# A fused convolution, attention and mixture-of-experts kernel: GpSimd in the planner's clock, and the experts' products summed by halves

## The chip, the cores and the metric

The kernel runs on one core of a Trainium2 chip. A core has a matrix engine (TensorE, PE in the profile, with its weight loads as PEld), a vector engine (VectorE, DVE), a scalar engine for activation functions (ScalarE, ACT), a general engine (GpSimd, POOL) and a queue engine that issues DMA transfers (SyncE, SP). Each engine executes its own instructions in the order in which they were written; engines wait for each other on semaphores. Operands lie in the on-chip memory SBUF (128 partitions) or in the accumulator banks of PSUM, which TensorE writes. The metric is device time in microseconds (us), the median of several runs.

## The reference, cut to what matters

The input is four images of 64 x 64 pixels and 128 channels. Layer 0 is a gated residual block with two 3 x 3 convolutions and a strictly causal attention over the 4096 pixels of an image; layer 1 is 16-head attention without a mask over the same 4096 tokens, a gated feed-forward network of width 344, and a mixture of experts in which each token takes the best 2 of 8 experts:

```python
# layer 0
c1 = conv_same(jax.nn.elu(x), W1, b1)
c2 = conv_same(c1, W2, b2)
a, b = jnp.split(c2, 2, axis=-1)
c3 = a * jax.nn.sigmoid(b)
# ... attention with q, k of 4 columns and v of 16, added to c3
# layer 1, t = tokens
scores = jnp.einsum('bqhd,bkhd->bhqk', q, k)      # 16 heads of 8
probs = jax.nn.softmax(scores, axis=-1)
attn = jnp.einsum('bhqk,bkhd->bqhd', probs, v)
h = x + attn @ wo
ffn = jax.nn.silu(h @ w1) * (h @ w3) @ w2
# experts
top_p, top_i = jax.lax.top_k(router_probs, 2)
expert_out = jnp.einsum('bnd,edc->bnec', x, expert_w) + expert_b
out = jnp.einsum('bnk,bnkc->bnc', top_p, jnp.take_along_axis(expert_out, top_i[..., None], axis=2))
```

The largest work is the exponential of layer 1's scores: 4 images x 16 heads x 4096 x 4096.

## The kernel before, in words

**Attention steps.** Tokens are cut into 8 chunks of 512 queries and 32 tiles of 128 keys, heads into 4 groups of 4. A *segment* is one image, group and chunk; it goes over up to 32 key tiles. A step of a segment is one key tile for four heads: four score matmuls on TensorE into two PSUM tiles (`s`, of three in rotation), two exponentials of 128 x 1024 on ScalarE (`e<-s`), and four value matmuls that add to a PSUM sum (`acc<-e,vg`). The value matmuls of a step are issued two steps later.

**Polynomial beside.** In segments that go over all 32 key tiles, key tile 20 is not given to ScalarE. Class `Beside` (L930) computes its exponential on VectorE: per head a score matmul into the single bank `m` (`m<-qx,f_kx`), a scaling out of the bank (`ey<-m`), and then eight SBUF operations of 128 x 512 (`em<-ey`, `eg<-em,ey`, `em<-em`, `ey<-eg`, three of `ey<-ey,eg`, and last `ey<-ey,em`). The eight wait in a list, `beside_todo`, and are issued a few at a time by `beside_work`. When all four heads are done, two *half products* (`half`; `acc<-ey,vg` in the profile, four matmuls each) add the tile to the sum. `rested` (L936 to L949) lets them begin only after two turns have passed since then.

**Fillers.** Between the steps the loop inserts pieces of other work through the same bank `m`: the next image's convolutions (in Winograd form: GpSimd makes the row terms `r` and column terms `v`, and the sums `both` and `less`; VectorE takes the products out of the bank as `sd`, `sums`, `t`), layer 0's attention, the queries and keys of layer 1, and the *last part* of a finished chunk (`last_part`, L1057): output projection, feed-forward network, normalization, router and experts. In the experts' stage each of a chunk's four token tiles gets two bank-fulls of products of four experts each; VectorE multiplies them by their gates into `by_e` (128 x 8 x 128), and then sums over the experts: one `tensor_reduce` on a rearranged view, so that its innermost step is 128 elements, into `added`, which is added to `t`.

**What sets the order.** The order of every engine is written out by hand in one loop (its last lines are L1490 to L1494). A pass is a *turn*, booked at 1.81 us (`turn_at`). Each turn issues one attention step, at most an insertion or two (a filler piece, a unit or a half product of the polynomial), the values of an older step, and then polynomial operations as long as VectorE's booked time `dve_at` stays under `turn_at + 2.5`. The function `dve_time` (L140) moves `dve_at` on with every VectorE operation by an estimate of its duration, and `bank_at` with those that read the bank `m`; pieces that need the bank are inserted only when `bank_at` has passed. GpSimd has no such clock. The clocks exist only while the program is built. Class `InOrder` (L93) records every operation through one line, L113, so in the profile all of them have that line, and groups are told apart by the names of their tiles.

At the end, when no attention step is left, the remaining fillers (here the last parts of the last two chunks) run alone: this is the *tail*.

Of the kernel before, what the change touches and what calls it, by code (L numbers as in the profile page):

```python
# [12 lines left out]
ALU = mybir.AluOpType  # L13
AX = mybir.AxisListType

P = 128
C = 128
# [10 lines left out]
NSLOT = P // SLOT  # L28
# [97 lines left out]
def fast_path(ctx: ExitStack, tc: tile.TileContext, a: dict, where: dict, out: bass.AP, verdict):  # L126
# [6 lines left out]
    nc = tc.nc  # L133
    x = a["x"]
    B = x.shape[0]
    pe, act, pool, sp = (InOrder(tc, e) for e in (nc.tensor, nc.scalar, nc.gpsimd, nc.sync))

    turn_at, dve_at, bank_at = [0.0], [0.0], [0.0]

    def dve_time(name, args):  # L140

        aps = [x for x in args if hasattr(x, "shape")]
        from_bank = any(x.name.startswith("m_") or x.name == "m" for x in aps)
        from_sums = any(x.name.startswith("acc") for x in aps)
        in_sbuf = not any(x.space == bass.MemoryType.PSUM for x in aps)
        took = max(int(np.prod(x.shape[1:])) for x in aps[:2]) / 960.0
        if in_sbuf and name in ("tensor_scalar", "tensor_copy"):
            took *= 0.5
        if name == "tensor_reduce" and aps[1].ap[-1][0] != 1:
            took *= 1.8  # L150
        begins = turn_at[0] + (0.95 if from_bank else 1.75 if from_sums else 0.0)
        dve_at[0] = max(dve_at[0], begins) + 0.07 + took
        if from_bank:
            bank_at[0] = dve_at[0]

    dve = InOrder(tc, nc.vector, dve_time)

    const = ctx.enter_context(tc.tile_pool(name="f_const", bufs=1))
    big = ctx.enter_context(tc.tile_pool(name="f_big", bufs=1))
# [11 lines left out]
    def m_tile():  # L171
        return ps_m.tile([P, QB], FP, tag="m", name="m")
# [7 lines left out]
    def chunk(tag, name=None):  # L180
        return wk.tile([P, QB], FP, tag=tag, bufs=CHUNKS.get(tag, 1), name=name or tag)
# [4 lines left out]
    def by_k(ap):  # L186
        return ap.rearrange("p (k c) -> p k c", k=4)
# [4 lines left out]
    def bank():  # L192
        return s_tile()[:, :QB] if alone[0] else m_tile()
# [153 lines left out]
    def halves(ps, lhs, rhs, size=P):  # L347

        for h in range(2):
            cols = slice(h * QB // 2, (h + 1) * QB // 2)  # L350
            product(ps[:size, cols], lhs, rhs[:, cols])
            if h == 0:
                yield 0.46, "held"
# [576 lines left out]
    class Beside:  # L930


        def __init__(self, seg, n, qx, vg):
            self.seg, self.kt, self.qx, self.vg = seg, seg.beside[n], qx, vg
            self.place = 8 * seg.place(self.kt // 8) + self.kt % 8
            self.e, self.units, self.halves, self.ready, self.rested, self.age = [], 0, 0, 0, 0, 0  # L936
            self.due = [2 + 3 * i for i in range(NSLOT)] + [22, 24]

        def can(self):
            if self.units < NSLOT:  # L940
                return len(beside_todo) < 10
            return self.halves < 2 and self.ready == NSLOT and self.rested > 1

        def late(self):
            return self.age > self.due[self.units + self.halves]

        def step(self):
            self.age += 1
            self.rested += self.ready == NSLOT  # L949

        def piece(self):
            if self.units < NSLOT:
# [6 lines left out]
        def unit(self, j):  # L959
            ps = m_tile()  # L960
            r = slice(j * SLOT, (j + 1) * SLOT)
            pe.matmul(
                ps,
                lhsT=kx[r, self.place * P : (self.place + 1) * P].bitcast(FR),
                rhs=self.qx[r, :].bitcast(FR),
                start=True,
                stop=True,
            )
            y = chunk("ey")
            self.e.append(y)  # L970
            dve.tensor_scalar(y, ps, LOG2E, None, ALU.mult)
            low, a = [], [-((-1) ** k) * POWER[k] / float(np.float32(POWER[5])) for k in range(5)]

            def round_off():
                low.extend([chunk("em"), chunk("part", "eg")])
                dve.tensor_scalar(low[0], y, TO_WHOLE + EXPONENT, None, ALU.add)

            def fraction():
                dve.scalar_tensor_tensor(low[1], low[0], TO_WHOLE + EXPONENT, y, ALU.subtract, ALU.subtract)

            def to_power():
                whole = low[0].bitcast(mybir.dt.int32)
                dve.tensor_scalar(whole, whole, 23, MANTISSA, ALU.logical_shift_left, ALU.bitwise_or)

            def first():
                dve.scalar_tensor_tensor(y, low[1], a[4], low[1], ALU.add, ALU.mult)

            def term(k):
                return lambda: dve.scalar_tensor_tensor(y, y, a[k], low[1], ALU.add, ALU.mult)

            def last():
                dve.scalar_tensor_tensor(y, y, a[0], low[0], ALU.add, ALU.mult)
                self.ready += 1

            beside_todo.extend([(0.35, round_off), (0.6, fraction), (0.35, to_power), (0.6, first)])
            beside_todo.extend([(0.6, term(3)), (0.6, term(2)), (0.6, term(1)), (0.6, last)])

        def half(self, h):
# [7 lines left out]
                    stop=False,  # L1006
                )

    def beside_work(until):
        while beside_todo and dve_at[0] + beside_todo[0][0] <= until:  # L1010
            beside_todo.pop(0)[1]()

    def beside_rest(seg):
# [43 lines left out]
    def last_part(b, c):  # L1057
# [30 lines left out]
        for m in range(4 * len(FCH)):  # L1088
            k, n = divmod(m, len(FCH))
# [25 lines left out]
        shape = [P, 4, NE]  # L1115
# [48 lines left out]
        for k in range(4):  # L1164
            tk = t[:, k * C : (k + 1) * C]
            by_e = wk.tile([P, NE, C], FP, tag="two", bufs=1, name="by_e")
            for half in range(2):
                ps = bank()
                yield from halves(ps, yT[:, k * P : (k + 1) * P], we_f[:, half * QB : (half + 1) * QB])
                dve.tensor_tensor(  # L1170
                    by_e[:, 4 * half : 4 * half + 4, :],
                    by_k(ps),
                    gate[:, k, 4 * half : 4 * half + 4].unsqueeze(2).to_broadcast([P, 4, C]),
                    ALU.mult,
                )
                if half == 1:
                    added = chunk("w", "added")[:, :C]
                    dve.tensor_reduce(added, by_e.rearrange("p e c -> p c e"), AX.X, ALU.add)
                    dve.tensor_tensor(tk, tk, added, ALU.add)
                fetch_following(b, c)  # L1180
                yield 0.46, "stop"
        ps = bank()
# [157 lines left out]
    jobs = []  # L1340
# [107 lines left out]
    while True:  # L1448
        turn_at[0] += EXPS
        if steps_in:  # L1450
            do_step(steps_in.pop(0))
        else:
            step = next(steps, False)
            if step is False:
                break
            waiting = step is None
            if waiting:
                finish(0)
            else:
                do_step(step)  # L1460
        b = now[0]
        if batches[b].second == NQ and len(batches) == b + 1 and b + 1 < B:
            Batch(b + 1)
            begun = 0
            while begun < len(fillers) and (fillers[begun][2] in fetching or fillers[begun][2] is None):
                begun += 1
            fillers.insert(begun, [first_attention(b + 1, batches[b + 1]), PREPARE, None, False])

        rate = 1.0
        if batches[b].second == NQ:  # L1470
            later = PREPARE * (B - len(batches)) + LAST * (last_parts_left[0] - 1)
            rate = (sum(part[1] for part in fillers) + later) / max(1, sum(steps_left) - 40)
        credit = min(3.0, credit + rate)
        left = ahead + EXPS - SCORES - (VALUES if len(undone) > 2 else 0.0)
        free = bool(fillers) and fillers[0][3]
        turn = not quiet[0] and free and not waiting
        if turn:
            took = insert()
            credit -= took
            left -= took  # L1480
        can = [job for job in jobs if job.can() and (left >= PIECE or job.late())]
        empty = bank_held[0] or bank_at[0] <= turn_at[0] + 0.5 or batches[b].second < NQ
        if can and empty and not (quiet[0] or bank_held[0] or steps_in or waiting):
            can[0].piece()
            left -= PIECE
        elif not turn and (waiting or not quiet[0] and empty and credit > 0.0 and (left >= PIECE or credit > 1.5)):
            took = insert()
            credit -= took
            left -= took
        ahead = min(max(left, 0.0), AHEAD)  # L1490
        finish(2)
        for job in jobs:
            job.step()
        beside_work(turn_at[0] + 2.5)  # L1494
    finish(0)
    alone[0] = True
    run_alone([(r for part in fillers for r in part[0])], lambda: False)
# [717 lines left out]
```

## Time and profile before

| what | value |
|---|---|
| median of 4 runs | 8134.53 us (8131.57 to 8137.83) |
| profiled execution, its own time | 8133.86 us |
| its span, first to last instruction | 8132.0 us |
| mean granted TensorE clock | 0.989 of full |
| ScalarE busy; of it the exponentials `e<-s` | 7690.2 us; 7624.5 us in 8256 instructions |
| TensorE busy | 7854.2 us |
| VectorE busy; of it `added<-by_e` | 4902.3 us; 256.0 us in 128 instructions |
| GpSimd busy | 675.4 us |
| ScalarE idle before `e<-s`, until `s` was there | 199.5 us in 132 waits, the longest 13.9 |

A line of the groups reads: source line, engine, operation, output tile `<-` input tiles, partitions x elements, `x` count, then busy us and mean ns of one, then the idle time of the engine just before them and what ended it. A line of the timeline reads: start in us from the start of the span, duration, engine, line, operation, tiles, `x` the number of instructions merged into it; in brackets the idle time before it and what ended it. `s<-qx,f_kx` are the score matmuls, `acc<-e,vg` the value matmuls, `m<-...` every product that goes through the bank `m`.

### The profile page before, as it was taken

The page shows a single profiled execution, that of the slowest core. Times are in us where ns is not written, and L with a number is a line of the kernel's source. Part 1 is how long each engine was busy: PE and PEld are TensorE (multiplying, and loading weights), DVE is VectorE, ACT ScalarE, POOL GpSimd, SP SyncE. Part 2 cuts the span into 40 slices and gives each one's busy share as a digit, 9 for nine tenths or more (in the row PEclk, how much of TensorE's full clock was granted, in tenths as well). Part 3 has the DMA queues.
Part 4 walks back from the last instruction along what each step waited for, and adds up shares of the span by engine and source line. Part 5 has one row for each costly group of instructions (what it writes and reads, how often), then busy time and mean ns, then how long its engine had stood idle before and what let it go on. Part 6 is the DMA issues. An engine that isn't in the chain of part 4 may idle for free. (4 is left out here: it accounts for less than half of the span.)

```text
span 8132.0 us, 177112 instructions
## 1 busy us (share of the span) xinstructions
PE 7854.2 (97%) x73465; PEld 2454.5 (30%) x73465; DVE 4902.3 (60%) x9033; ACT 7690.2 (95%) x8459; POOL 675.4 (8%) x592
## 2 busy tenths in 40 slices
PE   7999999999999999999999999999999999999997
PEld 3232222223322222333322222223233333333333
DVE  4333556463666766656666766666666666666666
ACT  1899999999999999999999999999999999999995
POOL 1211211100012111000001211000000000000000
PEclk9999999999999999999999999999999999999998
DMA  2221010111100101111010011101101111111221
GB/s 72 67 68 65 26 55 31 56 34 61 37 29 13 48 25 42 35 43 39 24 39 28 18 43 42 48 25 47 33 23 55 51 45 49 58 51 44 71 79 33
DMA packets 332338, 356.53 MB, mean 44 GB/s; under 512 B 146083, under 2 KB 222339, under 8 KB 331523
## 3 DMA queue, kind: packets, MB, share of 16 engines
q1 hardware_dynamic: 327507, 343.35, 13.4%
q8 instruction: 578, 9.47, 0.5%
q10 hardware_dynamic: 4016, 1.77, 0.1%
q14 instruction: 237, 1.94, 0.1%
HBM read 209.24 MB, written 135.79 MB: 42 GB/s over the span
## 5 line engine op out<-in xcount | busy, mean ns | idle before, releaser
L113 ACT ACTIVATE e<-s 128x1024 f32<-128x1024 f32 x8256 | 7624.5, 1086 | 208.9 <-PE s L113 199.5
L113 PE MATMUL acc<-e,vg 128*9 128x512 f32 x31872 | 4228.8, 596 | 1.6 <-DVE at L113 1.6
L113 PE MATMUL s<-qx,f_kx 32*128 32x512 f32 (+2 forms) x16512 | 2674.6, 496 | 38.2 <-DMA f_kx<-d_k 20.7
L113 PEld LDWEIGHTS s<-qx,f_kx 32*128 32x128 f32 (+1 forms) x16512 | 1082.3, 182 | 3886.2 <-ACT e L113 3619.2
L113 DVE SCALAR_TENSOR_TENSOR ey<-ey,eg 128x512 f32<-128x512 f32 x1344 | 954.8, 710 | 37.4
L113 PEld LDWEIGHTS acc<-e,vg 128*9 128x9 f32 x31872 | 726.0, 90 | 797.9 <-issue 405.4
L113 PE MATMUL m<-v,f_wino 128*32 128x256 f32 x5376 | 432.9, 394 | 44.6 <-DVE sd L113 25.5
L113 DVE COPY at<-acc 128x512 f32<-128x512 f32 x131 | 90.6, 692 | 621.3 <-PE acc L113 613.0
L113 DVE TENSOR_SCALAR ey<-m 128x512 f32<-128x512 f32 x448 | 306.4, 684 | 56.8 <-PE m L113 53.8
L113 PE MATMUL m<-f_we,y2T 128*32 128x256 f32 x3840 | 308.0, 393 | 28.7 <-DVE by_e L113 28.7
L113 DVE SCALAR_TENSOR_TENSOR eg<-em,ey 128x512 f32<-128x512 f32 x448 | 323.4, 722 | 13.3
L113 DVE SCALAR_TENSOR_TENSOR ey<-ey,em 128x512 f32<-128x512 f32 x448 | 321.1, 717 | 9.9
L113 POOL TENSOR_TENSOR rs<-ve,f_minus_half 128x4 f32<-128x4 f32 x64 | 65.2, 1018 | 3138.0 <-DVE ve L113 3138.0
L113 DVE SCALAR_TENSOR_TENSOR ey<-eg 128x512 f32<-128x512 f32 x448 | 320.7, 716 | 0.0
L113 POOL TENSOR_TENSOR v<-r 128x1024 f32<-128x1024 f32 x112 | 219.6, 1967 | 1132.2 <-PE m L113 1131.8
L113 DVE COPY sd<-m 128x512 f32<-128x512 f32 x168 | 115.8, 689 | 278.4 <-PE m L113 277.7
L113 DVE TENSOR_REDUCE added<-by_e 128x128 f32<-128x1024 f32 x128 | 256.0, 2000 | 5.3 <-DMA d_g<-turned 0.9
L113 DVE TENSOR_TENSOR by_e<-m,gates 128x512 f32<-128x512 f32 x240 | 165.1, 688 | 132.1 <-PE m L113 130.6
L113 PE MATMUL m<-hT,f_fw 128*32 128x256 f32 (+1 forms) x2640 | 228.5, 391 | 0.0
L113 PE MATMUL m<-qx,f_kx 32*128 32x512 f32 x448 | 194.9, 435 | 28.4 <-DVE ey L113 19.9
L113 POOL TENSOR_TENSOR t<-t,h 128x512 f32<-128x512 f32 x32 | 45.1, 1408 | 2080.6 <-DVE h L113 2080.6
L113 DVE TENSOR_SCALAR em<-ey 128x512 f32<-128x512 f32 x448 | 202.9, 453 | 13.2
(260 smaller groups left out, 4260.6 us busy)
## 6 DMA issues: line engine op xcount, KB each, us to landing
f_kx<-d_k SPq DMA_DIRECT2D x139, 512.0 KB
qx<-d_q SPq DMA_DIRECT2D x152, 256.0 KB
d_q<-two SPq DMA_DIRECT2D x64, 512.0 KB
d_a<-at SPq DMA_DIRECT2D x128, 256.0 KB
vg<-d_v SPq DMA_DIRECT2D x32, 576.0 KB
d_k<-two SPq DMA_DIRECT2D x32, 512.0 KB
d_v<-vc SPq DMA_DIRECT2D x32, 288.0 KB
xe<-in_x_dram SPq DMA_DIRECT2D x32, 256.0 KB
```

The source lines that it names most:

```text
L113: made = op(*args, **kw)
```

## The change

GpSimd gets a clock like VectorE's (`pool_time`, `pool_at`): each of its operations is booked from half a microsecond after its turn, for 0.65 us and 1.25 ns per element of a partition. In `dve_time` an operation without PSUM operands that begins before `pool_at` is booked 0.75 us longer. `beside_work` gets a second argument: unless a polynomial is late for its age, its operations are not issued while GpSimd is booked. The half products no longer wait for two turns; they may go when the clock has the polynomial done by 0.4 us after the start of the turn (`done_at`). The sum over the experts becomes three additions in place, of halves (4, 2 and 1 experts wide), and the first eighth is added to `t`.

```diff
-    pe, act, pool, sp = (InOrder(tc, e) for e in (nc.tensor, nc.scalar, nc.gpsimd, nc.sync))
-
-    turn_at, dve_at, bank_at = [0.0], [0.0], [0.0]
+    pe, act, sp = (InOrder(tc, e) for e in (nc.tensor, nc.scalar, nc.sync))
+
+    turn_at, dve_at, pool_at, bank_at = [0.0], [0.0], [0.0], [0.0]
+
+    def pool_time(name, args):
+
+        aps = [x for x in args if hasattr(x, "shape")]
+        if aps and name != "dma_start":
+            took = 0.65 + 1.25e-3 * int(np.prod(aps[0].shape[1:]))
+            pool_at[0] = max(pool_at[0], turn_at[0] + 0.5) + took
...
         begins = turn_at[0] + (0.95 if from_bank else 1.75 if from_sums else 0.0)
+        if in_sbuf and max(dve_at[0], begins) < pool_at[0]:
+            took += 0.75
         dve_at[0] = max(dve_at[0], begins) + 0.07 + took
...
-    dve = InOrder(tc, nc.vector, dve_time)
+    dve, pool = InOrder(tc, nc.vector, dve_time), InOrder(tc, nc.gpsimd, pool_time)
...
-            self.e, self.units, self.halves, self.ready, self.rested, self.age = [], 0, 0, 0, 0, 0
+            self.e, self.units, self.halves, self.ready, self.done_at, self.age = [], 0, 0, 0, 0.0, 0
...
-            return self.halves < 2 and self.ready == NSLOT and self.rested > 1
+            return self.halves < 2 and self.ready == NSLOT and self.done_at <= turn_at[0] + 0.4
...
             self.age += 1
-            self.rested += self.ready == NSLOT
...
                 self.ready += 1
+                self.done_at = dve_at[0]
...
-    def beside_work(until):
+    def beside_work(until, beside_pool=True):
         while beside_todo and dve_at[0] + beside_todo[0][0] <= until:
+            if not beside_pool and max(dve_at[0], turn_at[0] + 0.5) < pool_at[0]:
+                break
             beside_todo.pop(0)[1]()
...
-                    added = chunk("w", "added")[:, :C]
-                    dve.tensor_reduce(added, by_e.rearrange("p e c -> p c e"), AX.X, ALU.add)
-                    dve.tensor_tensor(tk, tk, added, ALU.add)
+                    for n in (4, 2, 1):
+                        dve.tensor_tensor(by_e[:, :n], by_e[:, :n], by_e[:, n : 2 * n], ALU.add)
+                    dve.tensor_tensor(tk, tk, by_e[:, 0], ALU.add)
...
-        beside_work(turn_at[0] + 2.5)
+        beside_work(turn_at[0] + 2.5, any(job.age > 3 * job.units + 4 for job in jobs if job.halves < 2))
```

## The prediction

> **What bounds the kernel now.** I read the page's head and its costliest groups first, then busy time by stage, then the list of waits, then the timeline at the longest waits.
>
> ```profile
> span 8132.0 us, 177112 instructions
> PE 7854.2 (97%) x73465; PEld 2454.5 (30%) x73465; DVE 4902.3 (60%) x9033; ACT 7690.2 (95%) x8459; POOL 675.4 (8%) x592
> ...
> L113 ACT ACTIVATE e<-s 128x1024 f32<-128x1024 f32 x8256 | 7624.5, 1086 | 208.9 <-PE s L113 199.5
> ...
> L113 DVE SCALAR_TENSOR_TENSOR ey<-ey,eg 128x512 f32<-128x512 f32 x1344 | 954.8, 710 | 37.4
> ...
> L113 DVE TENSOR_REDUCE added<-by_e 128x128 f32<-128x1024 f32 x128 | 256.0, 2000 | 5.3 <-DMA d_g<-turned 0.9
> ```
>
> Busy time in three stages (columns: stretch, its length, then busy us of PE, PEld, DVE, ACT, POOL):
>
> ```profile
> 0.00:200.00 200.00, 149.41 (x594) 71.43 (x594) 87.28 (x207) 30.13 (x41) 27.85 (x57) 0.92 0.24 73
> 200.00:8034.00 7834.00, 7649.39 (x72648) 2342.13 (x72644) 4753.35 (x8689) 7655.48 (x8412) 642.92 (x530) 0.99 0.14 43
> 8034.00:8132.00 98.00, 55.45 (x235) 40.91 (x227) 61.64 (x137) 4.63 (x9) 4.61 (x6) 0.76 0.08 22
> ```
>
> The middle stage is the kernel. In it ScalarE's exponentials run back to back: 7655.5 us of 7834.0. So a change to the stream can win at most the 178.5 us in which ScalarE stands still, and VectorE's 60% is worth nothing by itself. ScalarE stands still when TensorE, which works in order and is as full, is held by a VectorE result. The longest such place (timeline):
>
> ```profile
> 2376.04 8.96 POOL L113 TENSOR_TENSOR v<-r 128x1024 f32<-128x1024 f32 x4
> ...
> 2379.38 1.77 DVE L113 SCALAR_TENSOR_TENSOR ey<-ey,em 128x512 f32<-128x512 f32 x1
> ...
> 2381.19 2.04 DVE L113 TENSOR_SCALAR em<-ey 128x512 f32<-128x512 f32 x1
> 2383.26 2.29 DVE L113 SCALAR_TENSOR_TENSOR eg<-em,ey 128x512 f32<-128x512 f32 x1
> 2385.59 0.43 DVE L113 TENSOR_SCALAR em<-em 128x512 int32<-128x512 int32 x1
> ...
> 2388.15 1.11 PE L113 MATMUL m<-f_consts,pos 128*128 128x128 f32 x4 [8.00 <-DVE pos L113]
> ...
> 2391.92 1.94 ACT L113 ACTIVATE e<-s 128x1024 f32<-128x1024 f32 x2 [9.05 <-PE s L113]
> ```
>
> While GpSimd works, polynomial instructions that take 0.43 or 0.69 us take 1.8 to 2.3. The convolution's `pos` queues behind them, TensorE waits 8.00 us for it, ScalarE 9.05. Over the whole trace 151 polynomial instructions overlap a GpSimd transfer and take 88.8 us more than their undisturbed kind; they lie in 65 clusters, and ScalarE gaps of over 0.25 us inside or within 7 us after a cluster sum to 62.0 us. The other gaps (DMA 21, the router's small VectorE operations before `by_e` 26, and the rest) have other causes.
>
> **The change, part by part.** The profiled execution took 8133.86 us: its span of 8132.0 and 1.9 around it; it lies 0.7 under the median of the four runs, 8134.53. The number of passes of the planner's loop (turns) is 4127 in both programs, and every engine does the same work but for the sums; what changes is the order.
>
> *1. Polynomial kept out of GpSimd's times.* For each of the 65 clusters I took the turns in which its polynomial instructions were issued and counted what the new order issues in the same turns around the same GpSimd operation: 352 fall to 211 in all, but at the costly places far more: 9 to 1 at 2371 us (ScalarE gap 9.05), 7 to 0 at 892 (5.81), 4 to 0 at 2505 (4.67), 5 to 2 at 959 and at 2571 (4.73 and 5.06), 8 to 3 at 1033 (4.07), 4 to 0 at 4830 (3.55). Each cluster's gap times the share of its instructions that goes gives -42.7 us. Bounds: -62.0 if all of it goes; -15 if GpSimd's clock is wrong (rival 3). I take -42.7, worked out from the places themselves.
>
> *2. Half products sooner.* The polynomial's result is used in two pieces by TensorE (`acc<-ey`, the half products). Before, these waited until two turns had passed; of 112 segments none had fewer than three turns between the turn that issues the last polynomial instruction and the first half product. Now the planner's clock decides: 27 segments have one turn, 18 two, 22 three, 45 more. The clock counts 0.60 us for an instruction that takes 0.69 and 0.03 to the next, and 0.34 for 0.43, so in dense stretches VectorE is later than it says. At 2160 us (timeline) the orders of both kernels are the same for 26 turns up to here:
>
> ```profile
> 2161.14 0.93 PE L113 MATMUL s<-qx,f_kx 32*128 32x512 f32 x4
> 2162.01 1.05 PE L113 MATMUL acc<-e,vg 128*9 128x512 f32 x8
> ...
> 2163.03 0.69 DVE L113 SCALAR_TENSOR_TENSOR ey<-ey,em 128x512 f32<-128x512 f32 x1
> ```
>
> The new order puts the half product between these `s` and `acc`; the last `ey` ends at 2163.72, 1.64 us after `s`, and the fourth of the half product's matmuls reads it: 1.64 less 0.28 for the three in front is a stall of 1.36. Behind the stalled matmul wait the `acc` products and the next `s`, and for these ScalarE; a turn with an inserted piece leaves TensorE no slack (at 6585.65 us the starts of `s`, piece, `acc` and the next `s` lie 0.44, 0.45 and 0.97 apart, 1.86 in all; ScalarE's pair of exponentials takes 1.85). Taking for each of the 27 the lateness that the nearest segment end of this trace had gives 41.9 us, for the 18 1.9; the old order's own exposure is 4.5 (it shows at 2788 as a TensorE wait of 2.09). Upper bound +39.3. Lower bound -4.5, its own waits gone and no new one: earlier use cannot win more, as no work is removed. In five of the 27 the orders agree for 21 turns or more ahead, and those alone make 14.2. Of the other 22 (27.7) I take half, because their lateness holds collisions that part 1 removes. 14.2 + 13.9 + 1.4 - 4.5 = **+25**.
>
> *3. Sums by halves.* Per token tile the strided reduce of 2.00 us becomes three additions of 512, 256 and 128 elements. No such trio is in the trace; its nearest rows are SBUF additions of these sizes: `an<-an,per` 0.685, `sums<-sd` 0.425 undisturbed, `t<-t,added` 0.292, with 0.035 between: 1.47. In the tail VectorE is the chain: eight reduces there of about 1.90 give 8 x 0.43 = **-3.4** (bounds: 0 if the additions pay a wait between them, -4 without their gaps). In the stream 120 lie beside the attention and win nothing. They can cost: the planner's clock counts the trio at 1.14, so it thinks 0.85 us freed where 0.53 is, and issues polynomial instructions into the difference. Followed through one last part (6591 to 6604 us), a `by_e` comes 0.3 and another 0.2 late, and a present wait of 0.21 goes: +0.3 in 30 such parts is 9 at most; TensorE's direct waits for `by_e`, 28.7 us in all, could also shrink by a few. Taken **+4**, bounds -4 to +9.
>
> A rule of the Trainium skill speaks against this part: the page "VectorE: DVE Perf Modes", in its rules for kernel authors, advises few operations, since each pays its own drain, and its tier table gives the reduce one element per cycle. A reduce of 1024 elements at that rate plus a fixed part would be about 1.2 us by estimate from the page, less than three additions, and the tail would grow by 2 us. This trace's `added` row, strided, shows 2.00, so the row decides.
>
> *4. Where the stream stops.* The new order does the transpose of `h` and its copy to `hT` before the last attention product instead of after: 0.66 + 0.82 = **-1.5** in the tail. The start differs by nothing up to turn 301.
>
> *5. GpSimd's penalty in the clock* (0.75 for SBUF operations of VectorE in its time) only moves insertions; 1380 of 4127 turns differ on TensorE. Nothing is removed and the waits not named above (about 100 us) can fall either way; I count 0 and keep 15 both ways.
>
> Sum: -42.7 + 25 - 3.4 + 4 - 1.5 = -18.6; 8133.9 becomes 8115.3, as a median **8116**.
>
> **The rivals.**
>
> 1. *The half products eat the gain (slower).* For: the measured lateness above; the granted clock falls to half for 3.4 us after many waits of this size (at 2036 a wait of 2.26 became a ScalarE gap of 3.47), about 1.7 us lost each time. The upper 39.3 with 15 such spells is 64: -42.7 - 3.4 - 1.5 + 4 + 64 = +20, 8155. It decides from about 60 us in these waits on. Against: at 5608 a wait of 2.25 left the clock full, and from turn 3250 on (a fifth of the stream) the measured lateness is at most 0.1.
>
> 2. *The gain is whole.* The lateness of the half products was itself made by collisions: -62 - 5 + 10 = -57, 8077. For: at 2776 four `h` instructions of 0.34 took 4.85 together beside GpSimd's `r`, and the greatest lateness, 6.2, follows. Against: those are layer-norm instructions, which are not moved, and the case at 2160 has no collision.
>
> 3. *The change does not do what it says.* The planner books GpSimd at the turn of issue, but GpSimd starts when its inputs are there: 79 of 366 transfers in the stream start over 2 us before their turn's products, the `r` at 2776 by 13 turns. Then the polynomial avoids empty times and meets the real ones: -15 - 5 + 25 + 4 = +9, 8143. Against: the clusters with large gaps nearly all belong to operations issued in the turn where they ran.
>
> **How the numbers follow.** No change from before can be told within 0.2%, 16.3 us: 8118.3 to 8150.8. The forecast has 0.42, with its own range 8098 to 8132 (part 2 between 8 and 41): two thirds of it faster, 0.28, one third within the bound, 0.14. Rival 2 has 0.20, faster. Rival 3 has 0.16: 0.09 within, 0.07 slower. Rival 1 has 0.20, slower. 0.02 is left for a gain or a loss from reordering alone, half each way. Faster 0.49, same 0.23, slower 0.28. For eight in ten the range runs from rival 2's place, 8075, to just under rival 1's, 8152; of the bounds the whole -62 with part 5's -15 (8052) and rival 1 with its +15 (8170) lie outside.
>
> **What the changed profile would show.** Right: ScalarE's idle before `e` down from 208.9 to some 190; the mean of `ey<-ey,eg` down from 710 ns towards 695; the 9.05 at 2382 and the 5.81 at 898 gone; new TensorE waits for `ey` before `acc<-ey`, 30 us or so in place of 4.2; the tail after the last exponential 5 us shorter; no `added`, and additions on `by_e` of 0.69, 0.43 and 0.29. Wrong: `acc<-ey` waits under 10 us (part 2 was too dear, rival 2) or over 55 with more half-clock spells (rival 1); a mean of `ey<-ey,eg` above 704, so that collisions stayed (rival 3); an addition in place on `by_e` of over 0.8 us; or a new long wait at an operation that none of the parts names.

## The result and the profile after

The changed kernel takes 8143.3 us (median of 32 runs, 8138.1 to 8150.2); the kernel before took 8134.5 in 52 runs beside it (8125.7 to 8143.3). The ratio is 1.0010, 95% interval 1.0005 to 1.0015: slower by a thousandth, about 8 us, where a gain of 18.6 was forecast. The profiled execution has a span of 8139.7, 7.7 more than before. From the page of the changed kernel:

```profile
span 8139.7 us, 177397 instructions
PE 7863.2 (97%) x73465; PEld 2454.9 (30%) x73465; DVE 4804.0 (59%) x9289; ACT 7690.3 (94%) x8459; POOL 670.9 (8%) x592
...
L113 ACT ACTIVATE e<-s 128x1024 f32<-128x1024 f32 x8256 | 7626.7, 1085 | 224.3 <-PE s L113 216.6
...
L113 DVE SCALAR_TENSOR_TENSOR ey<-ey,eg 128x512 f32<-128x512 f32 x1344 | 954.0, 710 | 36.7
```

VectorE has 98 us less to do and ScalarE the same work as before, but ScalarE's idle time before `e` went up, from 208.9 to 224.3. Busy time in the three stages (columns as before; the last exponential ends at 8047.1, before at 8034.4):

```profile
0.00:200.00 200.00, 149.97 (x610) 71.44 (x614) 87.18 (x207) 31.62 (x42) 27.86 (x57) 0.93 0.25 73
200.00:8046.00 7846.00, 7658.86 (x72624) 2343.83 (x72620) 4658.50 (x8930) 7653.29 (x8409) 639.44 (x530) 0.99 0.14 43
8046.00:8139.70 93.70, 54.41 (x239) 39.65 (x231) 58.30 (x153) 5.38 (x10) 3.56 (x5) 0.77 0.08 23
```

The stream is 12.7 us longer and the tail after the last exponential 5.1 shorter (92.5 from 97.6, to the end of the span). So the loss is in the stream. Which results TensorE waits for is the next view: its waits, as engine, tile that was to be written, releasing engine and tile, then us in total, times, longest. Before:

```profile
PE m L113 <- DVE sd L113: 34.1, 29, 4.5
PE m L113 <- DVE ey L113: 33.3, 41, 2.9
PE m L113 <- DVE by_e L113: 28.7, 37, 2.3
...
PE m L113 <- DVE pos L113: 8.4, 2, 8.0
...
PE acc L113 <- DVE ey L113: 4.2, 2, 2.1
```

After:

```profile
PE m L113 <- DVE ey L113: 50.5, 69, 4.6
PE acc L113 <- DVE ey L113: 38.7, 22, 4.6
PE m L113 <- DVE by_e L113: 28.4, 23, 2.3
...
PE m L113 <- DVE sd L113: 3.7, 9, 0.8
```

The waits of the convolution at the bank for VectorE (`sd`, `pos`) are nearly gone, as the keep-out is meant to do; that it is the keep-out is shown below, where it stands alone. In their place stand two others: half products that wait for the end of their polynomial (`acc` for `ey`, 4.2 to 38.7), and products into the bank `m` that wait until the polynomial's scaling `ey<-m` has read it (33.3 to 50.5).

For ScalarE I sorted every gap of over 0.3 us before an exponential of the stream by the TensorE operation that had stood still longest just ahead of it; "collisions" are gaps with over 0.8 us of polynomial time lost beside GpSimd in the 8 us ahead.

| ScalarE gaps in the stream, us | before | after |
|---|---|---|
| collisions of the polynomial with GpSimd | 61.5 | 7.5 |
| half products, `acc<-ey,vg` | 4.8 | 53.4 |
| experts' products, `m<-f_we,y2T` | 26.2 | 41.8 |
| the polynomial's score products, `m<-qx,f_kx` | 13.7 | 23.9 |
| `m<-f_eb,g` | 0 | 4.5 |
| transfer of keys, `s<-qx,f_kx` | 21.3 | 22.3 |
| all idle time of ScalarE in the stream | 178.5 | 192.7 |

The 14.2 between the sums, less 1.5 of ScalarE's work that now lies before 200 us (31.62 in place of 30.13), is the 12.7 of the stream.

**The collision that went.** The place at 2376 to 2392 us of the kernel before, with its gap of 9.05, is found again by its GpSimd instructions: the same four `v<-r` run at 2370.20 in the changed kernel:

```profile
2370.20 8.63 POOL L113 TENSOR_TENSOR v<-r 128x1024 f32<-128x1024 f32 x4
...
2371.34 1.34 DVE L113 SCALAR_TENSOR_TENSOR pos<-neg,pos 128x512 f32<-128x512 f32 x1 [2.39 <-ACT neg L113]
...
2372.60 2.11 DVE L113 TENSOR_SCALAR pos<-xe 128x512 f32<-128x512 f32 x1
...
2374.82 2.23 DVE L113 SCALAR_TENSOR_TENSOR pos<-neg,pos 128x512 f32<-128x512 f32 x1
...
2377.83 0.66 PE L113 MATMUL m<-f_consts,pos 128*128 128x128 f32 x4 [0.89 <-DVE f_e_band L113]
...
2379.34 2.97 DVE L113 SCALAR_TENSOR_TENSOR ey<-ey,eg 128x512 f32<-128x512 f32 x2
...
2380.00 11.21 ACT L113 ACTIVATE e<-s 128x1024 f32<-128x1024 f32 x12 [0.86 <-PE s L113]
```

While the four run, to 2378.83, no polynomial instruction runs on VectorE. `pos` itself meets GpSimd and takes up to 2.23, but no polynomial stands ahead of it: TensorE waits 0.89 before the product of `pos` where it waited 8.00, and ScalarE 0.86 where it waited 9.05. Polynomial instructions still meet GpSimd's next work (two take 2.97 in place of 1.4, from 2379.34), with no long wait behind them: twelve exponentials run without a stop. So the mean of `ey<-ey,eg` could stay at 710 ns although the gaps went.

**The wait that came.** The longest new one, in the timeline of the changed kernel:

```profile
2747.55 2.42 DVE L113 TENSOR_SCALAR h<-xt,mv,rs 128x128 f32<-128x128 f32 x2
...
2750.88 0.61 PE L113 MATMUL acc<-ey,vg 128*9 128x256 f32 x4
...
2754.31 2.14 DVE L113 SCALAR_TENSOR_TENSOR ey<-ey,eg 128x512 f32<-128x512 f32 x3
2756.48 0.69 DVE L113 SCALAR_TENSOR_TENSOR ey<-ey,em 128x512 f32<-128x512 f32 x1
...
2757.23 0.60 PE L113 MATMUL acc<-ey,vg 128*9 128x256 f32 x1 [4.55 <-DVE ey L113]
...
2760.78 3.93 ACT L113 ACTIVATE e<-s 128x1024 f32<-128x1024 f32 x4 [7.65 <-PE s L113]
```

VectorE is late first because of the layer norm: four `h` instructions, of which the two last are shown, took 4.8 us together beside GpSimd, and the planner's clock, which has GpSimd done before them, books 0.14 for each. It issues the half product one turn after the polynomial. TensorE stands 4.55 at the fourth matmul, ScalarE 7.65. At the place that the prediction traced, 2160 us before, the wait came almost as worked out, 1.16 for 1.36:

```profile
2155.46 0.38 PE L113 MATMUL acc<-ey,vg 128*9 128x256 f32 x1 [1.16 <-DVE ey L113]
...
2157.44 2.87 ACT L113 ACTIVATE e<-s 128x1024 f32<-128x1024 f32 x3 [1.49 <-PE s L113]
```

**The small one that repeats.** Most last parts of the late phase, from 6240 us on, have a gap like this:

```profile
6601.37 1.48 DVE L113 TENSOR_TENSOR by_e<-by_e 128x512 f32<-128x512 f32 x3
...
6601.58 0.39 PE L113 MATMUL m<-qx,f_kx 32*128 32x512 f32 x1
...
6602.88 0.29 DVE L113 TENSOR_TENSOR t<-t,by_e 128x128 f32<-128x128 f32 x1
6603.09 0.54 DVE L113 RECIPROCAL sums<-sums 128x64 f32<-128x64 f32 x1
6603.56 0.63 DVE L113 TENSOR_SCALAR ey<-m 128x512 f32<-128x512 f32 x1
...
6604.24 0.64 PE L113 MATMUL m<-f_we,y2T 128*32 128x256 f32 x8 [0.83 <-DVE ey L113]
...
6606.26 2.90 ACT L113 ACTIVATE e<-s 128x1024 f32<-128x1024 f32 x3 [0.66 <-PE s L113]
```

A score product of the polynomial has filled the bank at 6601.97. Its reader `ey<-m` stands behind the three additions, `t` and a reciprocal and ends at 6604.19; the next experts' product needs the bank and waits 0.83. By the planner's clock the bank was free: it has `ey<-m` done at the start of the turn that issues the next product.

### The profile page after: what moved, and what is told of

The parts are those of the page before. It is cut to its first block, busy times and chain, and to the rows that moved or that the text cites. A ratio compares the mean times of both kernels' runs of the same rounds, so it can differ in the third digit from the quotient of the medians.

```text
span 8139.7 us, 177397 instructions
## 1 busy us (share of the span) xinstructions
PE 7863.2 (97%) x73465; PEld 2454.9 (30%) x73465; DVE 4804.0 (59%) x9289; ACT 7690.3 (94%) x8459; POOL 670.9 (8%) x592
## 5 line engine op out<-in xcount | busy, mean ns | idle before, releaser
L113 ACT ACTIVATE e<-s 128x1024 f32<-128x1024 f32 x8256 | 7626.7, 1085 | 224.3 <-PE s L113 216.6
L113 PE MATMUL s<-qx,f_kx 32*128 32x512 f32 (+1 forms) x16512 | 2668.0, 497 | 39.3 <-DMA f_kx<-d_k 20.9
L113 DVE TENSOR_SCALAR em<-em 128x512 int32<-128x512 int32 x448 | 196.0, 438 | 10.2
```

Of the source, the lines that this page charges most:

```text
L113: made = op(*args, **kw)
```

## The experiments

Each kernel was timed beside the kernel before on the same chip (which took 8134.9 there for the first four, 8134.5 for the next four and 8135.3 for the last four). The first four kernels take the change apart with the planner's clock as it is; the next four touch the clock or its margin; the three after them repeat the taking apart with the clock set right, and the last one moves the insertions. Most were run four times, and the runs of one kernel lie 2 to 17 us apart. Tails are given to the end of the span; expectations that speak of a tail of 87 or of one 12.6 longer count it to the last instruction of an engine, 5 to 8 us less.

### Which part does what

**The changed kernel with the old rule of two turns:**

```diff
-            return self.halves < 2 and self.ready == NSLOT and self.done_at <= turn_at[0] + 0.4
+            return self.halves < 2 and self.ready == NSLOT and self.rested > 1
```

> The changed kernel with one thing put back: the half products wait for two turns again, instead of for the planner's clock. Theory: the waits of the half products (ScalarE gaps before acc<-ey, 4.8 us before and 55 after) are what took the gain, so they fall back to about 5 and the time falls by 45 to 50, to about 8095. Rival (the dense order loses the same time wherever it is put: VectorE is late in any case, and with the half products later another bank wait takes their place): within 10 us of the changed kernel, 8133 to 8150.

Measured: 8117.1 (8110.2 to 8121.8), ratio 0.9976 (0.9967 to 0.9986). The half-product gaps fell to 7.0 and the stream ends 37.6 us sooner than the changed kernel's, at 8009.6. But the tail is longer by 14.6 (107.1 from 92.5): when the stream stops, this order has 2.3 us of pieces left in one last part and all 18.3 of the next, where the changed one has 16.8 of the next. So the new rule costs 26 us here; the theory's 8095 took no account of the tail.

**The kernel before with the sums by halves alone:**

```diff
-                    dve.tensor_reduce(added, by_e.rearrange("p e c -> p c e"), AX.X, ALU.add)
-                    dve.tensor_tensor(tk, tk, added, ALU.add)
+                    for n in (4, 2, 1):
+                        dve.tensor_tensor(by_e[:, :n], by_e[:, :n], by_e[:, n : 2 * n], ALU.add)
+                    dve.tensor_tensor(tk, tk, by_e[:, 0], ALU.add)
```

> The kernel before with the three additions for the one reduce, and nothing else. Theory: the tail gives 3.4 back, but the planner books 0.85 us freed per token tile where 0.53 is, and the waits for by_e before m<-f_we grow from 26 us to about 40: 8140 to 8148. Rival (these new waits are made by the other two parts and only show at by_e): the tail's gain alone, 8131.

Measured: 8166.5 (8158.7 to 8175.6), ratio 1.0044 (1.0027 to 1.0060), more than either expectation. The stream of the profiled run, the fastest of the four at 8158.7, is 28 us longer, with the waits for the bank's reader `ey` nearly doubled:

```profile
PE m L113 <- DVE ey L113: 60.7, 78, 2.9
```

**The kernel before with GpSimd's clock, its penalty and the keep-out alone** (two turns, strided reduce):

```diff
+            pool_at[0] = max(pool_at[0], turn_at[0] + 0.5) + took
...
+        if in_sbuf and max(dve_at[0], begins) < pool_at[0]:
+            took += 0.75
...
+            if not beside_pool and max(dve_at[0], turn_at[0] + 0.5) < pool_at[0]:
+                break
```

> The kernel before with GpSimd's clock, its penalty and the polynomial kept out of its times, but with the two-turn rule and the one reduce. Theory: the ScalarE gaps with collisions (61 us before, 8 after) go here too, and the densely packed polynomial gives some 5 to 10 back at m<-qx: 8085 to 8095. Rival (order alone decides, gains are given back at once): 8125 to 8140.

Measured: 8118.7 (8117.3 to 8124.3), ratio 0.9982 (0.9972 to 0.9991), between the theory's range and the rival's. The collisions' gaps fell from 61.5 to 1.4, all of them, but the stream ends only 27.1 us sooner: gaps at `m<-f_we` rose from 26.2 to 49.2 and at `m<-qx` from 13.7 to 32.6, and the tail is 10.6 longer (108.2). In its waits the trade is plain:

```profile
PE m L113 <- DVE ey L113: 47.5, 59, 4.7
PE m L113 <- DVE by_e L113: 44.0, 23, 2.3
...
PE m L113 <- DVE sd L113: 1.4, 5, 0.5
```

**The kernel before with the half products' new rule alone:**

```diff
-            return self.halves < 2 and self.ready == NSLOT and self.rested > 1
+            return self.halves < 2 and self.ready == NSLOT and self.done_at <= turn_at[0] + 0.4
...
+                self.done_at = dve_at[0]
```

> The kernel before with only the half products' rule changed to the planner's clock. Theory: some 40 to 50 us of new waits before acc<-ey and nothing won: 8175 to 8185. Rival (the early half products are harmless in the old order, and late only because the kept-out polynomial is packed more densely): 8130 to 8145.

Measured: 8181.7 (8178.4 to 8184.1), ratio 1.0058 (1.0041 to 1.0075). The gaps at half products went from 4.8 to 44.5, the others stayed, and the time rose by 47: as expected.

Alone, the three parts give -16, +32 and +47 us, a sum of 63; together they give 9. So they do not add up: each new order has waits of its own. What the places followed above have in common is that something stands ready by the planner's VectorE clock and is not ready in the trace.

### The clock

The traces give the length of additions on SBUF: 692 ns for 512 elements, 425 for 256, 292 for 128, that is 1.04 ns an element (1/960 us, which the planner's clock books too) and 0.16 fixed, with some 0.034 between two. The clock books 0.07 fixed. The clock with 0.19 is called the right clock below. It is right for these sizes; for a reciprocal of 64 elements it still books 0.26, where the trace has 0.545.

**The changed kernel with 0.19 in place of 0.07, and the thresholds of the polynomial's list to match:**

```diff
-        dve_at[0] = max(dve_at[0], begins) + 0.07 + took
+        dve_at[0] = max(dve_at[0], begins) + 0.19 + took
...
-            beside_todo.extend([(0.35, round_off), (0.6, fraction), (0.35, to_power), (0.6, first)])
+            beside_todo.extend([(0.46, round_off), (0.73, fraction), (0.46, to_power), (0.73, first)])
...
-            beside_todo.extend([(0.6, term(3)), (0.6, term(2)), (0.6, term(1)), (0.6, last)])
+            beside_todo.extend([(0.73, term(3)), (0.73, term(2)), (0.73, term(1)), (0.73, last)])
```

> The changed kernel, with the planner's VectorE clock set to what the traces show: 0.19 us beside the elements of each operation in place of 0.07 (512 elements: 0.723 by the clock, 0.726 from start to start in the trace; before 0.603), and the polynomial's bookings 0.73 and 0.46 for 0.60 and 0.35. Theory: the new waits come from a clock that is ahead of VectorE. Then the ScalarE gaps at half products fall from 55 us to under 15, those at f_we from 42 to about 26 and those at m<-qx from 24 to about 14, as in the kernel before: some 65 us off the stream. The planner also inserts less: where it leaves the stream, the changed kernel has 16.8 us of pieces left in its current last part; this one has 8.3 of one part and 18.3 of the next left. The two-turn kernel had 2.3 and 18.3 left and a tail 12.6 us longer, so this tail is taken as some 30 us longer. In all 8105 (8090 to 8120). Rival: the clock is not the cause and each new order has its own waits of that size: the waits do not fall by half, and the longer tail makes 8150 to 8175.

Measured: 8053.5 (8047.3 to 8056.5), ratio 0.9896 (0.9879 to 0.9912). 90 us faster than the changed kernel, well beyond the theory. Gaps at `m<-f_we` and `m<-qx` are not back at their old level, they are gone; all idle time of ScalarE in the stream comes to 94 us in place of 192.7. The tail is 121, longer by 28 as expected. The half-product gaps were expected under 15 and are 27.8.

**The changed kernel, half products one turn later:**

```diff
-            return self.halves < 2 and self.ready == NSLOT and self.done_at <= turn_at[0] + 0.4
+            return self.halves < 2 and self.ready == NSLOT and self.done_at <= turn_at[0] - 1.4
```

> The changed kernel, with half products allowed only when the clock has passed the polynomial's end by 1.4 us (before: from 0.4 us ahead of it), that is one turn later. The planner stops at the same place as the changed kernel does (16.8 us of pieces left in the current part), so the tail stays at about 87. Theory: nearly all of the loss is the lateness at one-turn places, most of it under 2 us: the ScalarE gaps at half products fall from 55 to about 20, the rest of the stream stays: 8143 - 35 = 8108 (8100 to 8118). Rival: as in the two-turn kernel a part of that comes back as waits at f_we and m<-qx (11 us there), and the longer polynomial wait costs slots: 8120 to 8140.

Measured: 8095.9 (8091.9 to 8097.0), ratio 0.9950 (0.9933 to 0.9967). That is below the theory's range. Half-product gaps are 20.4, 33 less; the rest of ScalarE's idle time in the stream fell by some 17 us, spread over many kinds of gap; the stream stops at the same place in its pieces and the tail is 94.7. So with a margin for the clock's error the change, otherwise as it is, is 39 us faster than the kernel before.

**The changed kernel with only the three additions booked right:**

```diff
                         dve.tensor_tensor(by_e[:, :n], by_e[:, :n], by_e[:, n : 2 * n], ALU.add)
+                        dve_at[0] += 0.12
```

> The changed kernel, with each of the three additions booked 0.12 us longer, so that the trio is 1.50 on the planner's clock as it is in the trace (1.14 before). Only this booking is changed. Theory: the new ScalarE gaps at f_we and f_eb (30.7 us before with m<-c, 47.5 after) come from polynomial instructions issued into time that the trio really takes; they fall by 10 to 17 and the time with them: 8126 to 8134. Rival: the gaps come from the trio standing where the reduce stood with the bank's reader behind it, or from the new order as such, and stay within 5 us: 8140 to 8146.

Measured: 8138.0 (8130.6 to 8143.4), ratio to before 1.0001 (0.9992 to 1.0011). Gaps at `m<-f_we` 39.5 from 41.8, at `f_eb` 0.3 from 4.5. The median lies between theory and rival, and the gaps moved by little, as the rival has it: the booking of the trio is a few us of it, not the cause.

**The changed kernel with two turns and the right clock:**

> The changed kernel with the old rule of two turns for the half products and with the calibrated VectorE clock (0.19 us for 0.07, bookings 0.73 and 0.46). Beside the two-turn kernel of before (8117) only the clock differs. Theory: its gaps at f_we (48) and m<-qx (29) fall to the level of the kernel before (26 and 14), 37 us less in the stream; it leaves 8.5 and 18.3 us of pieces for the tail in place of 2.3 and 18.3, which costs some 18: 8098 (8088 to 8108). Rival: those gaps do not come from the clock, and the tail is paid: 8130 to 8140.

Measured: 8045.2 (8042.6 to 8054.3), ratio 0.9889 (0.9873 to 0.9906). Beside the two-turn kernel at 8117.1 only the clock differs: 72 us, where the theory gave 19. TensorE's waits for `by_e` and for `ey` with the old clock, in that kernel:

```profile
PE m L113 <- DVE ey L113: 53.3, 71, 4.6
PE m L113 <- DVE by_e L113: 43.1, 22, 2.3
...
PE acc L113 <- DVE ey L113: 4.2, 2, 2.1
```

With the right clock:

```profile
PE acc L113 <- DVE ey L113: 16.3, 9, 3.8
...
PE m L113 <- DVE ey L113: 0.7, 3, 0.3
```

Waits of `m` for `by_e` and for `sd` are no longer in the list. How it comes about is seen in the same situation as at 6601 above, in the timeline of this kernel:

```profile
6443.83 1.48 DVE L113 TENSOR_TENSOR by_e<-by_e 128x512 f32<-128x512 f32 x3
6444.26 0.64 PE L113 MATMUL m<-f_we,y2T 128*32 128x256 f32 x8
6445.34 0.29 DVE L113 TENSOR_TENSOR t<-t,by_e 128x128 f32<-128x128 f32 x1
6445.55 0.54 DVE L113 RECIPROCAL sums<-sums 128x64 f32<-128x64 f32 x1
6446.12 0.64 PE L113 MATMUL m<-f_we,y2T 128*32 128x256 f32 x8
6446.83 0.69 DVE L113 TENSOR_TENSOR by_e<-m,gates 128x512 f32<-128x512 f32 x1 [0.74 <-PE m L113]
```

No score product of the polynomial is put in while VectorE is behind: the planner inserts only when `bank_at[0] <= turn_at[0] + 0.5`, and with the longer bookings the test no longer lets one through here. VectorE now waits for TensorE here (0.74), not TensorE for VectorE. The price is fewer insertions, so more pieces are left for the tail (8.5 us of one last part and 18.3 of the next; the tail is 123 us).

The half-product gaps that are left (25.8) lie at segment ends: 10 of the 11 segments in which the half products are issued in the very turn of the polynomial's last instruction, because the segment is over and `beside_rest` forces both out, have such a gap.

### Taken apart again, with the right clock

Three more kernels make a square with the last one. All have two turns and the same pieces left at the end. Each is the kernel of before with the clock's edit above: the first with that alone, the second with the sums' edit as well, the third with the keep-out's.

> The kernel before with the calibrated VectorE clock alone (0.19 us for 0.07, bookings 0.73 and 0.46). With the two next kernels and the one at 8045 it makes a square: keep-out of the polynomial yes or no, sums by halves yes or no, all with the right clock, the old rule of two turns and the same pieces left for the tail (8.5 and 18.3 us). Theory: the wrong clock made the orders' own waits and the keep-out is worth what I priced it at, once these are gone: this kernel still has its 60 us of collisions and runs 43 to 55 over 8045: 8088 to 8100. Rival: the clock does everything, because an order with true times has slack where GpSimd disturbs: 8040 to 8058.

> The kernel before with the calibrated clock and the sums by halves, no keep-out. Alone and with the old clock the sums cost 32 us. Theory: that was the booking of 1.14 us for a trio that takes 1.50, and the whole order with it; with the right clock they cost nothing in the stream and win 0.43 in each of some nine reduces of the tail: 4 below the kernel with the clock alone, within 8 either way. Rival: the additions cost by their place in front of the bank's next reader: 20 or more above the kernel with the clock alone.

> The kernel before with the calibrated clock, GpSimd's clock, its penalty and the keep-out; the strided reduce stays. Theory: the same as the kernel at 8045 but for the sums, 4 above it: 8049 (8043 to 8056), and 43 to 55 below the kernel with the clock alone. Rival on the sums: they lose with the right clock too, and this kernel is at 8015 to 8035; rival on the keep-out: it is worth under 15 against the clock alone.

| with two turns, us | old clock | right clock |
|---|---|---|
| before | 8134.5 | 8073.9 (8067.5 to 8074.9) |
| sums by halves | 8166.5 | 8065.4 (8064.3 to 8066.4) |
| keep-out | 8118.7 | 8051.9 (8049.2 to 8053.0) |
| both | 8117.1 | 8045.2 (8042.6 to 8054.3) |

The ratios to before of the three new ones are 0.9924 (0.9907 to 0.9940), 0.9915 (0.9898 to 0.9932) and 0.9899 (0.9883 to 0.9916). With the right clock the parts add up: the sums give -8.5 and -6.7, the keep-out -22.0 and -20.2. The -6.7 alone is not clear of the spread: the runs with both and with the keep-out overlap, and the two kernels were timed on different chips. Neither theory nor rival on the keep-out was right: 43 to 55 was too much and under 15 too little. The kernel with the clock alone has 37.7 us of collisions' gaps in place of 61.5, the keep-out takes them to 4.0, and it gives back 22.4 of half-product gaps, the segment ends just named: the polynomial, kept out and truly booked, is more often not done when its segment is (3 segments with half products in the turn of the last instruction with the clock alone, 13 with the keep-out). The sums, which cost 32 us alone under the old clock, now win 7 to 9, in the expected 4 within 8.

**Two turns, right clock, insertions done sooner:**

```diff
-            rate = (sum(part[1] for part in fillers) + later) / max(1, sum(steps_left) - 40)
+            rate = (sum(part[1] for part in fillers) + later) / max(1, sum(steps_left) - 200)
```

> The kernel at 8045 (changed kernel, two turns, calibrated clock) with one number more: the rate at which pieces are inserted aims to be done 200 attention steps before the end in place of 40. The planner then leaves nothing of the last parts it has begun (before: 8.5 and 18.3 us of pieces). Theory: its tail of 123 us loses the one part and a half that ran in it, about 47 us for a part: some 50 us are left for the last part; the stream pays 27 us more of pieces, most of it beside ScalarE: plus 10 to 20. In all 7990 (7980 to 8010). Rival: TensorE at 98% has no room for the pieces, and the stream grows by as much as the tail shrinks: 8030 to 8050.

Measured: 8011.3 (8010.5 to 8013.7), ratio 0.9850 (0.9833 to 0.9866), just over the theory's range and the fastest of all. Its stream and its tail, in the columns of the stages above:

```profile
200.00:7943.50 7743.50, 7652.24 (x73000) 2352.66 (x72996) 4705.48 (x9000) 7644.28 (x8416) 648.16 (x532) 1.00 0.14 44
7943.50:8008.70 65.20, 28.91 (x139) 21.06 (x127) 31.20 (x82) 2.31 (x5) 2.41 (x3) 0.72 0.09 28
```

The tail is 57.9 us shorter than the 122.9 of the kernel at 8045 (65.0 from the end of the last exponential); the stream pays 21.4. The tail was expected at 50; a wait of 12.5 for `an`, which comes by a chain of transfers, is most of the difference by its size.

## Why the prediction was wrong

The median of 8143.3 lies inside the range given, 8075 to 8152, but the forecast was a gain of 18.6 and the result is a loss of 8, within the 0.2% that the prediction calls no change. Two steps failed: step 2, whose +25 came to +48.6, and step 5, taken as 0, which with step 3's +4 for the stream came to some +19. By the steps of the prediction, in ScalarE gaps of the stream:

| step | forecast | measured |
|---|---|---|
| 1 keep-out | -42.7 | -54.0 in collisions' gaps |
| 2 half products sooner | +25 | +48.6 at `acc<-ey` |
| 3 sums, in the tail | -3.4 | with step 4 together -5.1 |
| 3 sums, in the stream | +4 | see below |
| 4 stream's stop | -1.5 | in the -5.1 |
| 5 reordering | 0, up to 15 | some +30 at the bank's products, less some 11 at others |

*Step 1* had its mechanism right and was too careful: nine tenths of the gaps went, not seven. What failed is what the step did not ask: what is late next. Alone the keep-out removes 60.1 us of gaps and makes the kernel 16 us faster; 42 come back at `m<-f_we` and `m<-qx`, and 10.6 in the tail.

*Step 2* is the mis-sized term. Its own measured lateness gave 41.9 + 1.9 - 4.5 = 39.3; I took half of the 22 places with differing order, "because their lateness holds collisions that part 1 removes" (and wrote 1.4 in the sum where 1.9 had been measured). Part 1 does not remove them: it moves polynomial instructions. Of the 22 waits of TensorE at half products in the changed kernel, 11 (23 us) have other VectorE work slowed beside GpSimd just ahead (a layer norm's `h`, or `c<-t,c`), 10 (14 us) nothing slowed at all, and one a polynomial instruction. The second fault is that the step counted a wait of TensorE as the same loss of ScalarE: TensorE's waits came to 38.7 us, not above the 43.8 of lateness that was measured, but ScalarE lost 53.4 with them. So the stated upper bound was none, though rival 1 had a price for this part, 1.7 us for each spell of the clock at half. With 39.3 the sum would have been -4.3, "same".

*Step 3* was right in the tail: a token tile's sum there takes 1.52 from the first addition to `t` (8120.27 to 8121.79) where the reduce took 1.93 (8111.53 to 8113.46), eight times. That the trio is three instructions with three fixed costs, against which a rule of the Trainium skill spoke (the page "VectorE: DVE Perf Modes", rules for kernel authors), is visible, 0.16 each; but the strided reduce cost more still, so the row that decided was the right one. In the stream, the gaps at `m<-f_we` and `m<-f_eb` rose by 20.1 in place of 4, but this is not the trio's doing alone: the keep-out alone, with the old reduce, has 49.2 at `m<-f_we`, and adding the sums to it changes 8118.7 to 8117.1. The sums cost 32 only in the old order under the old clock; with the right clock the gaps at `m<-f_we` are gone with the trio and without it.

*Step 5* failed in size and in principle. I gave new orders an expectation of zero. But the old clock errs to one side: it thinks VectorE done 0.12 us too soon per instruction. It is argued from this, and not shown apart, that an order that packs more polynomial into fewer turns (keep-out), or more instructions into the same place (sums), is behind by more. The prediction had the error in hand ("counts 0.60 us for an instruction that takes 0.69 and 0.03 to the next"), and used it for the half products and the trio only. The experiments show that it was worth some 61 us in the kernel before already (8073.9, where the kernel before took 8135.3 beside it), more than any part of the change.

*The rivals.* Rival 1, the half products eat the gain, named the right mechanism. The gaps came to 53, near its point of 60, and the time between the forecast and its 8155. By its own mark it is not confirmed: TensorE's waits are 38.7, between the "30 us or so" of the forecast and the 55 of the rival. Rival 2 is refuted by its lower mark: the half products' lateness is there although the polynomial's collisions are not. That collisions lie behind half of it is true, but they are those of the layer norm and the copies, which the prediction had held against this rival. Rival 3 gives the time to the microsecond (8143), by luck, and its sign, a mean of `ey<-ey,eg` above 704, came true; yet its mechanism is refuted: collisions stayed, but at harmless places, and their gaps fell to 7.5. The mean of an instruction was the wrong mark for that; the waits for `sd` and `pos` were the right one.

That the planner's clock, ahead of VectorE, is the cause of these waits rests on four things together: only that constant and its thresholds were changed; the waits that went are those on results VectorE delivers late; a margin of one turn on the half products alone takes off 33 of their 53 us of gaps; and under the right clock the parts add up. An obvious rival, that the longer bookings help only by putting fewer pieces into the stream and more into the tail, does not explain the gain: the last kernel leaves nothing of a begun part to the tail, which is 65.0 us against 97.6 in the kernel before, and its stream has 99 us of idle ScalarE in place of 178.5. What is not shown is that 0.19 must be the true value: no kernel booked more than the trace has, so a planner that is simply more cautious may do as well or better. Which share belongs to the constant and which to the list's thresholds was not tried. Why the sums alone made the waits for `ey` rise from 33.3 to 60.7 was not followed place by place.

## What to carry to other kernels

Where a planner books an engine by an estimate, compare its bookings with the trace first, start to start and for each size: here 0.12 us per VectorE instruction was worth 60 us in the kernel before and 90 in the changed one, and the keep-out, built on the wrong clock, gave back 42 of the 60 us of gaps that it removed. When a wait is removed on an engine with a late queue, price what stands behind it in the same queue; the list of which tiles TensorE waits for, before and after, shows the trade in a few lines. A measured exposure is not halved without a place in the trace that shows the half, a wait of one engine is not the loss of the next until the trace shows the ratio (here 38.7 became 53.4), and a stream that stops with pieces left hands each of them to a tail where nothing runs beside it.

## What the runs showed of the hardware

- A VectorE addition of two SBUF tensors in float32 took 0.16 us and 1.04 ns an element, for 128, 256 and 512 elements alike (292, 425, 692 ns), and the next one began 0.034 later. A reciprocal does not follow this: 64 elements took 0.545 us, as the groups of the changed kernel show, where the planner books 0.14.

```profile
L113 DVE RECIPROCAL sums<-sums 128x64 f32<-128x64 f32 x32 | 17.5, 545 | 1.6 <-DMA sums<-d_a 1.6
```

- The polynomial's instructions beside GpSimd still lost some 60 us in the changed kernel (about 110 of them, 88.8 us and 151 before), and nearly all of it was free: the gaps of ScalarE with them came to 7.5. The page "SBUF — State Buffer" of the Trainium skill (section "SBUF: two separate sides") describes the ports that the two share as locked for a whole instruction; the trace agrees in so far as single polynomial instructions took up to 2.3 us in place of 0.69. At the places followed here, what such a loss cost depended on whether TensorE needed something behind it.
- A wait of TensorE at a half product cost ScalarE more than itself: 4.55 us became a gap of 7.65 at 2757, 1.16 became 1.49 at 2155. After the long one the granted clock was at half for a while (four score matmuls at 2759.89 took 0.80, at 2762.17 again 0.50); such spells make 112.6 us of the changed kernel's stream, in 24 spells, and 99.0 in 19 before.
